# A four-block attention and scan kernel: the scan block's 64 prefix tokens computed in an own pass beside the first two stages

## The chip, the core and the metric

The kernel runs on one core of a Trainium2 chip. A core has TensorE (PE in the profile; its weight loads are the row PEld), VectorE (DVE), ScalarE (ACT), GpSimd (POOL) and SyncE (SP, which issues most DMAs here). Each engine works through its own queue in order; semaphores make an operation wait for others. SBUF is the on-chip memory of 128 partitions, PSUM the smaller one that PE writes its results to. The metric is device time in microseconds (us): the median of 3 runs is 4272.25 (4264.49 to 4274.65).

## The reference

Four blocks in a row on x of 4 sequences x 512 tokens x 256 features, all in float32:

- Block 0: cross-attention (16 heads of 16) to a context of 64 tokens, then a feed-forward part.
- Block 1: self-attention (16 heads of 64), cross-attention, gated feed-forward part, each after a layer norm.
- Block 2, the scan block: a prefix of 64 tokens, computed from the context alone, is put ahead of the 512 tokens, and four layers of a selective state-space scan run over all 576. At the end the prefix is dropped.
- Block 3: self-attention (16 heads of 16), cross-attention, feed-forward part.

The part that matters:

```
p = silu(prepend_cond @ pre_w1) @ pre_w2            # 64 prefix tokens, from the context alone
h = concatenate([p, x], axis=1)
for l in range(4):
    h = h + mamba_block(rmsnorm(h, norm_w[l]), ...)
return rmsnorm(h, final_norm_w)[:, 64:, :]

# mamba_block, E = 512 channels e, 16 states s
xi, z = split(x @ in_proj);  xi = silu(conv4(xi) + cb)     # causal, 4 taps
dt, Bm, Cm = split(xi @ x_proj);  dt = softplus(dt @ dt_proj + b)
h_t = exp(dt_t * A) * h_(t-1) + dt_t * Bm_t * xi_t         # for each e and s
y_t = sum over s of h_t * Cm_t + xi_t * D
return (y * silu(z)) @ out_proj
```

The scan is causal, so the prefix tokens never depend on x. What the 512 tokens need of the prefix is, for each layer, the state after its last token (h at token 63, for each channel and state) and the last three inputs of the convolution.

## The kernel before

Tokens lie on partitions in blocks 0, 1 and 3 (X, 16 tiles of 128 tokens), features in the scan block (hT, 2 chunks of 128 features x 4 sequences x 576 tokens). Line numbers are those of the profile.

**Blocks 0 and 1.** `cross_stage` (L348) and `self_stage` (L530) write out the order of the work by hand. A `Pieces` object (L59) holds small pieces, each a group of matmuls on PE and an eviction that reads their PSUM bank; `work` (L78) issues the matmuls of the next piece, `evict` (L70) the evictions of those issued before. The self-attention goes through 64 groups of four 128x512 score tiles (and 4 more iterations for what trails). One iteration k: PE transposes half of group k-1 (L668, copied to SBUF by ACT at L671), then makes the scores of group k (L627); DVE takes the row maxima (L642) and ACT the exponentials (L646); PE multiplies with the values (L687) and does a piece; PE transposes the other half of k-1, which DVE copies (L673); DVE divides the exponentials of group k by their sums, in SBUF (L654, L656); PE multiplies and does another piece. POOL only raises variances to the power -1/2 for the layer norms (L311) and adds biases to X (L815). The eight big weights of blocks 0 and 1 pass through six slots of 1 MB (pool w8): Wq1, Wk1, Wv1 and Wo1 are loaded during block 0, Wq2 and Wk2 when W1 and W2 are done with, Wv2 and Wo2 at the end of the self-attention, Wpa, Wpg and Wf after it.

**Scan block** (`layer2`, L942). 16 units n, one for each layer and sequence; each has two pairs of channel chunks, and each pair 16 main steps: two chunks times 8 groups of two states. The main steps i run through all units without a stop, and one of them is, spread over the engines:

```
nc.gpsimd.tensor_mul(dBu[:, :, 1:], dtx ..., bmap[i // 2, 0][:, :, 1:])            # L1385, POOL
nc.scalar.activation(dA, dt[:, S:], AF.Exp, scale=A[:, l, m, s : s + 1])           # L1397, ACT, into PSUM
nc.scalar.copy(dBus[i][:, :, 0], h0[:, 2 * s2 : 2 * s2 + 2])                       # L1402, ACT
nc.vector.tensor_tensor_scan(to, dA, dBus.pop(i) ..., 0.0, ALU.mult, ALU.add)      # L1412, DVE
nc.vector.tensor_mul(hCs[i], dA, bmap[i // 2, 1])                                  # L1419, DVE, 3 of 4 steps
nc.gpsimd.tensor_mul(hCs[i], hCs[i], bmap[i // 2, 1])                              # L1423, POOL, 1 of 4 steps
```

PE then sums over the states by transposing into one PSUM tile (L1445). The rows of B and C that these need reach all partitions by DMAs from a scratch tile in DRAM (`maps`, L1378). Beside the main steps, generators advance twice a step: `front` (norm, input projection, convolution as four matmuls with diagonal weights, B, C and dt) for the unit after next, `step` for the next pair, `gate` and `gated` for z, the product with silu(z) and the output projection with its residual add (L1362). Two PSUM banks are shared among them through `need`, `bank` and `done`.

The prefix goes through all this as 64 more columns: projections and convolution work on two halves of 288 columns (L1096, L1107, L1127, L1203), and `step` holds the prefix scan of each chunk: 16 exponentials of 64 columns (L1228, ACT), dt·x·B as one product of 128x1040 (L1230, POOL), one scan of 128x1040 (L1237, DVE), both of whose operands lie in SBUF, and a copy of the last state (h0, L1245, POOL). In layers 0 to 2 there are also the product with C (L1248, POOL), its sum over states on PE (L1261), a gate (L1317, L1326) and 64-column matmuls for z and the output projection. The prefix embedding itself (L1012 to L1017) opens the block.

## Time and profile before

| what | value |
|---|---|
| median of 3 runs | 4272.25 us |
| the profiled execution's own time | 4271.5 us |
| its span, first to last instruction | 4269.7 us |
| block 0 (0 to 266 us): PE / DVE / ACT / POOL busy | 222.7 / 117.1 / 67.2 / 62.8 us |
| block 1, self-attention (266 to 930 us) | see the prediction |
| block 1, cross-attention (930 to 1160 us) | 196.4 / 123.1 / 48.1 / 6.0 us, clock 0.96 |
| block 1, feed-forward (1160 to 1350 us) | 180.9 / 50.9 / 32.1 / 21.3 us |
| scan block, lead-in (1350 to 1430 us) | 64.9 / 10.0 / 35.3 / 14.8 us |
| scan block, main steps (1430 to 3515 us) | see the prediction |
| block 3 (3570 to 4270 us) | 609.3 / 411.9 / 314.3 / 73.4 us |
| scan block: distance of the products with silu(z) (L1460), one for each pair | 65 us mostly, 48.5 to 68.1 |

The profile is of one execution. A group's line gives the source line, engine, operation, the tiles (output <- inputs), the shapes, how many; then the busy time in us and the mean duration of one in ns; then the engine's idle time just before these instructions and what ended most of it. The line of a source line gives durations as minimum/median/maximum. A line of the timeline gives start, duration, engine, source line and tiles, and in brackets the idle time ahead of it. An f32 matmul shows as two records, a transpose as one. The granted clock is the share of TensorE's full clock that its throttle passed.

### The profile page before, as it was taken

What the parts mean: (1) busy time and instruction counts of PE and PEld (TensorE: products, weight loads), DVE (VectorE), ACT (ScalarE), POOL (GpSimd) and SP (SyncE); (2) the same over time, 40 slices, a digit from 0 to 9 for tenths busy, and PEclk for the clock granted to TensorE, in tenths of its full rate; (3) what the DMA queues carried; (4) which work ended last, traced back from release to release, by engine and by line L of the source; (5) the groups of instructions that cost most, each with busy time, mean ns of one, the idle gap of its engine ahead of it and who ended that gap; (6) DMA issues with size and microseconds to landing.
All of it is one profiled execution on the core that took longest, in us unless ns stands there. A gap on an engine that the chain in (4) does not pass through costs nothing. (4 is left out here: it accounts for less than half of the span.)

```text
span 4269.7 us, 51401 instructions
## 1 busy us (share of the span) xinstructions
PE 3642.0 (85%) x19008; PEld 2467.8 (58%) x19008; DVE 3086.3 (72%) x3120; ACT 2336.6 (55%) x5236; POOL 2146.8 (50%) x1204
## 2 busy tenths in 40 slices
PE   7999999988899788888887888888878567888789
PEld 3555555556556566666666666666656444545446
DVE  5536666664521599999999999999998986666653
ACT  2334445431212777777776777767777644555322
POOL 2300000010000799999999999999888971000131
PEclk8999999999999888889888898888888668999999
DMA  2000000010000344344344443444443431000000
GB/s 97 1 19 1 1 1 1 8 41 1 2 0 11 112 147 142 137 145 150 122 149 135 141 157 121 147 138 137 159 139 120 157 104 54 1 1 1 1 6 15
DMA packets 102378, 322.53 MB, mean 76 GB/s; under 512 B 12848, under 2 KB 28784, under 8 KB 100080
## 3 DMA queue, kind: packets, MB, share of 16 engines
q1 hardware_dynamic: 100048, 317.04, 22.4%
q8 instruction: 151, 2.47, 0.2%
q10 hardware_dynamic: 2080, 2.20, 0.2%
q14 instruction: 99, 0.81, 0.1%
HBM read 315.92 MB, written 3.28 MB: 75 GB/s over the span
## 5 line engine op out<-in xcount | busy, mean ns | idle before, releaser
L1385 POOL TENSOR_TENSOR dBu<-dtx,bB 128x1022 f32<-128x1022 f32 x512 | 1282.5, 2524 | 18.1 <-DVE ps_dA L1412 10.9
L1397 ACT ACTIVATE ps_dA<-dt,A 128x512 f32<-128x512 f32 x1024 | 706.7, 690 | 442.1 <-DVE hC L1419 399.3
L1412 DVE TENSOR_TENSOR_SCAN ps_dA<-ps_dA,dBu 128x1024 f32<-128x1024 f32 x384 | 877.3, 2285 | 52.8 <-ACT ps_dA L1397 24.3
L1445 PE MATMUL ps_y<-ident,hC 128*128 128x128 f32 x3072 | 472.2, 307 | 48.8 <-DVE hC L1419 48.4
L1419 DVE TENSOR_TENSOR hC<-ps_dA,bC 128x1024 f32<-128x1024 f32 x384 | 469.1, 1222 | 25.3 <-PE ps_y L1445 0.4
L1445 PEld LDWEIGHTS ps_y<-ident,hC 128*128 128x128 f32 x3072 | 414.5, 162 | 103.4 <-DVE hC L1419 72.3
L646 ACT ACTIVATE pr<-ps_s,nm 128x512 f32<-128x512 f32 x512 | 344.8, 685 | 233.1 <-DVE nm L642 233.1
L642 DVE TENSOR_REDUCE nm<-ps_s 128x2 f32<-128x1024 f32 x256 | 301.5, 1219 | 207.9 <-PE ps_s L627 186.9
L1423 POOL TENSOR_TENSOR hP<-hP,bC 128x1024 f32<-128x1024 f32 x128 | 301.6, 2356 | 79.9 <-DVE hP L1412 77.7
L160 PE MATMUL ps_cv<-xp,w_dg 128*128 128x288 f32 x1024 | 305.3, 457 | 37.0 <-ACT xp L1127 24.9
L311 POOL TENSOR_TENSOR ln_rstd<-ln_rstd,const 128x4 f32<-128x4 f32 x20 | 20.3, 1016 | 594.6 <-DVE ln_rstd L310 539.2
L1412 DVE TENSOR_TENSOR_SCAN hP<-ps_dA,dBu 128x1024 f32<-128x1024 f32 x128 | 292.1, 2282 | 30.0 <-PE ps_y L1445 28.5
L668 PEld LDWEIGHTS ps_pt<-ident,pr 128*128 128x128 f32 x2048 | 233.6, 141 | 136.8 <-issue 81.6
L668 PE MATMUL ps_pt<-ident,pr 128*128 128x128 f32 x2048 | 275.8, 276 | 33.9 <-DVE pT L673 22.1
L160 PEld LDWEIGHTS ps_cv<-xp,w_dg 128*128 128x128 f32 x1024 | 216.9, 217 | 117.8 <-issue 19.3
L1237 DVE TENSOR_TENSOR_SCAN hp<-dAp,hp 128x1040 f32<-128x1040 f32 x64 | 244.0, 3813 | 54.3 <-ACT dAp L1228 49.8
L1228 ACT ACTIVATE dAp<-dt,A 128x64 f32<-128x64 f32 x1024 | 282.0, 338 | 0.0
L208 POOL MEMSET Vbd<- 128x1024 f32 (+1 forms) x3 | 5.4, 1804 | 490.9 <-PE ps_wo L160 490.9
L687 PE MATMUL ps_o<-pT,V 128*64 128x256 f32 (+1 forms) x2048 | 220.0, 391 | 0.0
L160 PE MATMUL ps_in<-hn,w_inx 128*128 128x288 f32 x512 | 164.8, 467 | 56.6 <-DVE hn L1096 51.9
L673 DVE COPY pT<-ps_pt 128x512 f32<-128x512 f32 x256 | 164.5, 682 | 58.9 <-PE ps_pt L668 58.3
L1445 PE MATMUL ps_y<-ident,hP 128*128 128x128 f32 x1024 | 159.4, 307 | 55.5 <-POOL hP L1423 55.5
(239 smaller groups left out, 6541.1 us busy)
## 6 DMA issues: line engine op xcount, KB each, us to landing
bB<-scr SPq DMA_DIRECT2D x256, 512.0 KB, 5.0
bC<-scr SPq DMA_DIRECT2D x256, 512.0 KB, 4.1
bc<-scr SPq DMA_DIRECT2D x16, 1040.0 KB, 6.6
X<-in_x SPq DMA_DIRECT2D x4, 512.0 KB, 7.1
w_L_W<-in_L_W SPq DMA_DIRECT2D x2, 1024.0 KB, 10.4
w_L_Wq<-in_L_Wq SPq DMA_DIRECT2D x2, 1024.0 KB, 9.0
w_L_Wo<-in_L_Wo SPq DMA_DIRECT2D x2, 1024.0 KB, 10.6
w_inx<-in_L_in SPq DMA_DIRECT2D x4, 512.0 KB, 6.1
```

The costliest lines, as they stand in the source:

```text
L160: nc.tensor.matmul(dst, a, b, start=(i == 0), stop=(i == n - 1))
L642: nc.vector.tensor_reduce(nm, ps, AX.X, ALU.max, negate=True)
L646: nc.scalar.activation(pr, ps[:, x, :], AF.Exp, bias=nm[:, x : x + 1], accum_out=rs[:, y : y + 1])
L668: nc.tensor.transpose(pp[:, t4, :], pr[:, t4 * P : (t4 + 1) * P], ident)
L1228: nc.scalar.activation(dAp[:, s, 1:], dt[:, 1:S1], AF.Exp, scale=A[:, l, m, s : s + 1])
L1237: nc.vector.tensor_tensor_scan(hpf, dAp.rearrange("p s t -> p (s t)"), hpf, 0.0, ALU.mult, ALU.add)
L1385: nc.gpsimd.tensor_mul(dBu[:, :, 1:], dtx[:, S1:].unsqueeze(1).broadcast_to([P, 2, T - 1]), bmap[i // 2, 0][:, :, 1:])
L1397: nc.scalar.activation(dA, dt[:, S:], AF.Exp, scale=A[:, l, m, s : s + 1])
L1412: nc.vector.tensor_tensor_scan(to, dA, dBus.pop(i).rearrange("p s t -> p (s t)"), 0.0, ALU.mult, ALU.add)
L1419: nc.vector.tensor_mul(hCs[i], dA, bmap[i // 2, 1])
L1423: nc.gpsimd.tensor_mul(hCs[i], hCs[i], bmap[i // 2, 1])
L1445: nc.tensor.matmul(y[:, j, k * P : (k + 1) * P], hC[:, s, j * P : (j + 1) * P], ident, is_transpose=True, start=False, stop=(2 * s2 + s == ...
```

## The change

The prefix tokens leave the scan block. A generator, `prefix_pass`, computes all four layers for the prefix tokens of all four sequences at once (256 columns), keeps the state after token 63 (h63) and the last three convolution inputs (tail), and is advanced in small turns from inside the cross-attention stage of block 0 and the self-attention of block 1. The scan block then works on 512 columns: its projections use one PSUM bank instead of two halves; the convolution's first three columns come from tail; the state at its start is exp(A·dt) h63 + dt·x·B for 16 states, in one ACT operation and three small POOL operations a chunk; silu is flushed at steps 10 and 15 of a unit.

The pass's matmuls are pieces of a queue of their own (`aside`), with a PSUM tile from the tag of the transposes (self-attention) or of the projections (block 0). The main turn of the pass and how it is called, cut to the core:

```
+        def product(i):                                  # POOL, 128x512
+            nc.gpsimd.tensor_mul(hb, dtx[:, m, :].unsqueeze(1).broadcast_to([P, 2, PT]), maps.pop((i, 0)))
+        def decay(i):                                    # ACT, 2 of 128x256
+            nc.scalar.activation(dA[:, s, :], dt[:, m, :], AF.Exp, scale=A[...])
+        def scan(i):                                     # DVE, 128x512, both operands in SBUF
+            nc.vector.tensor_tensor_scan(hb, dA, hb, 0.0, ALU.mult, ALU.add)
+        def behind(i):
+            nc.scalar.copy(h63[:, l, :, m, 2 * q : 2 * q + 2], hb...[:, :, :, S - 1])
+            if not more:                                 # more: layers 0 to 2
+                return
...
+            nc.gpsimd.tensor_mul(hb, hb, bC)
+            nc.gpsimd.tensor_add(ys[m], ys[m], hb)
...
+        for i in range(NB + (4 if more else 3)):         # NB = 32
+            if i < NB: product(i)
+            if i + 1 < NB: load(i + 1, 0)                # SP, 256 KB to all partitions
+            if more and 0 <= i - 2 < NB: load(i - 2, 1)
+            if 0 <= i - 1 < NB: decay(i - 1)
...
+            if 0 <= i - 2 < NB: scan(i - 2)
+            if 0 <= i - 3 < NB: behind(i - 3)
+            to().busy = i < NB + 2
+            yield
```

(Conditions that stand on two lines in the kernel are written on one here.) Its convolution is one multiply-add with bias and three multiply-adds on DVE for each chunk, over 256 columns. The tiles for xi, z, dt and dt·x lie in hT, which is free until the scan block. In the self-attention:

```
                 evict()
+                todo.go_on(1)
                 back = k and k <= K
                 if back:
                     transposes(k - 1, 0)
+                todo.work_aside()
                 if k < K:
                     scores(k)
                     softmaxed(k)
                 through_values(lead // 2)
+                evict(0)
+                if k % 2 or not todo.busy:
+                    todo.go_on(1)
+                todo.work_aside()
                 work()
                 evict()
                 if back:
                     transposes(k - 1, 1)
+                todo.go_on(1)
+                todo.work_aside()
+                through_values(lead // 2)
+                evict(0)
                 if k < K and wide:
                     divided(k)
-                through_values(lead // 2)
                 work()
```

After the last iteration, what is left of the pass is run to its end. In block 0 the stage takes one turn in each of its 19 iterations and one after every second of the 32 feed-forward matmul groups: 35 in all.

To make room in SBUF, the weight pool has four slots instead of six: two hold block 0's gelu outputs first, so Wq1, Wk1, Wv1 and Wo1 wait for the slots of W1, W2 and these; Wk2 and Wv2 are loaded at the end of the self-attention; Wq2, Wo2 and Wf get a pool of their own that is opened when the pass's memory is free, after the self-attention. In block 0 the norm of the attention output is written over it instead of into a tile of its own. A is computed at the start of the program.

In the scan block, of `step`:

```
-                    hp = pool.tile([P, NS, S1], F32, name="hp", tag="hp")
-                    for s in range(NS):
-                        nc.scalar.activation(dAp[:, s, 1:], dt[:, 1:S1], AF.Exp, scale=A[:, l, m, s : s + 1])
-                        if s == 3:
-                            nc.gpsimd.tensor_mul(hp, dtx[:, :S1]..., bc0[:, 0])
...
-                    nc.vector.tensor_tensor_scan(hpf, dAp..., hpf, 0.0, ALU.mult, ALU.add)
...
+                    nc.scalar.activation(h0, A[:, l, m, :], AF.Exp, scale=dt[:, 0:1])
+                    yield
+                    nc.gpsimd.tensor_mul(i0, b0, dtx[:, 0:1].broadcast_to([P, NS]))
+                    nc.gpsimd.tensor_mul(h0, h0, h63[:, l, b, m, :])
+                    nc.gpsimd.tensor_add(h0, h0, i0)
+                    nc.scalar.copy(dt[:, 0:1], far)
```

`prefix_sum` and `prefix_gated` are gone, and so are the 64-column matmuls for z and the output projection, and the 1 MB load of the prefix's B and C for each unit.

## The prediction

> **What bounds the kernel now.** I read the busy time by stretches first, since shares over the whole span mix stages with different limits. The columns are the stretch, its length, then busy us (instructions) of PE, PEld, DVE, ACT and POOL, the granted clock, the DMA share and GB/s.
> ```profile
> 266.00:930.00 664.00, 649.06 (x3320) 356.43 (x3320) 416.91 (x797) 312.95 (x763) 31.39 (x33) 1.00 0.03 9
> 1430.00:3515.00 2085.00, 1684.58 (x8693) 1298.39 (x8691) 1925.14 (x1152) 1512.14 (x3401) 1921.66 (x943) 0.84 0.42 139
> ```
> The first stretch is the first self-attention: PE is busy 649 of 664 us and POOL does nothing. The second is the scan block: DVE and POOL are both busy 92%, PE 81%. So work moves from a stage that DVE and POOL bound into one that PE bounds. Next, the groups of instructions, for what the prefix costs where it is.
> ```profile
> L1385 POOL TENSOR_TENSOR dBu<-dtx,bB 128x1022 f32<-128x1022 f32 x512 | 1282.5, 2524 | 18.1 <-DVE ps_dA L1412 10.9
> L1237 DVE TENSOR_TENSOR_SCAN hp<-dAp,hp 128x1040 f32<-128x1040 f32 x64 | 244.0, 3813 | 54.3 <-ACT dAp L1228 49.8
> L1228 ACT ACTIVATE dAp<-dt,A 128x64 f32<-128x64 f32 x1024 | 282.0, 338 | 0.0
> ```
> The prefix scan (L1237) means 3.81 us, while the main scan of nearly the same length (L1412) means 2.28. The timeline of DVE, then of POOL, at one such scan says why:
> ```profile
> 2200.45 3.52 DVE L1237 TENSOR_TENSOR_SCAN hp<-dAp,hp 128x1040 f32<-128x1040 f32 x1
> 2203.90 2.27 DVE L1412 TENSOR_TENSOR_SCAN ps_dA<-ps_dA,dBu 128x1024 f32<-128x1024 f32 x1
> ```
> ```profile
> 2199.43 2.37 POOL L1385 TENSOR_TENSOR dBu<-dtx,bB 128x1022 f32<-128x1022 f32 x1
> ...
> 2201.77 4.35 POOL L1385 TENSOR_TENSOR dBu<-dtx,bB 128x1022 f32<-128x1022 f32 x1
> ```
> The scan starts at 2200.45, ends 2.2 us after POOL's product ends (2201.8), and the next product lasts 4.35 instead of 2.36: they take turns. All 42 products over 2.5 us lie beside an L1237 scan. The main scan, which reads one operand from PSUM, never shows this. Last, one step of the self-attention (PE and DVE of the timeline):
> ```profile
> 502.42 1.04 PE L668 MATMUL ps_pt<-ident,pr 128*128 128x128 f32 x8
> ...
> 504.56 2.35 DVE L642 TENSOR_REDUCE nm<-ps_s 128x2 f32<-128x1024 f32 x2 [1.87 <-PE ps_s L627]
> ...
> 508.77 1.29 DVE L673 COPY pT<-ps_pt 128x512 f32<-128x512 f32 x2 [1.86 <-PE ps_pt L668]
> ...
> 511.16 0.88 DVE L656 TENSOR_SCALAR pr<-pr,rs 128x512 f32<-128x512 f32 x2
> 511.94 1.04 PE L668 MATMUL ps_pt<-ident,pr 128*128 128x128 f32 x8
> ```
> A step takes 9.5 us, and DVE ends its division (L656) just as PE needs it: DVE has two gaps of 1.9 us, both waits for PE.
>
> **Scan block: removed.** It has 16 units (4 layers x 4 sequences) of 2085/16 = 130.3 us; DVE is busy 1925/16 = 120.3 of each. Out of each go four L1237 scans, 244.0/16 = 15.25, less 0.08 each that the trace lets overlap: 14.9; the prefix gate (L1326, 24 x 0.27/16 = 0.4); the 64-column residual add (24 x 0.21/16 = 0.3); and four 288-column norm products of 0.50 become two of 512 at some 0.75 (L913, same operation and width): 0.5. DVE keeps 104.2. POOL keeps 120.1 - 8.8 (L1230) - 7.1 (L1248) - 42 x 2.0/16 = 5.2 (products no longer held up) - 1.4 (shorter dtx, no h copy) + 2.4 (12 tiny operations at the h copy's 0.20) = 100.0, plus its 9.7 idle: less than DVE, so DVE stays the bound. ACT loses 17.6 a unit, PE its prefix sums. DVE's 10 us idle a unit: waits for ACT's decays (24.3 us in all) and for dtx (14.9) should shrink, waits for PE's out-projection (39.9) stay. I take 8, so a unit is 112.2 and the block loses 18.1 x 16 = **290 us**. Bounds: idle 5 (-338) and 12 (-226).
>
> **Lead-in of the block.** The prefix embedding between 1343.6 and 1353.7 goes (10 us), and of the 24 us from the end of the first softplus (1403.7) to the first main product (1427.6), with 32 exps and two scans, some 4 stay. I take **-30**; bounds -15 and -38.
>
> **Added: how much work, and where it falls.** A layer of the pass has 32 main steps (36 turns, with the pipeline's ends) and 13 or 14 turns of projections. In the cross block there are 35 turns, and there a projection costs two turns: 22 go for embedding and head of layer 0, 13 for main steps. The self-attention gets 3 turns an iteration, 2.5 while main steps run: 23+36+36 = 95 three-product turns (38 iterations), 35 of the last layer (14), 40 others (13.4). That is 65 of 68 iterations, so nothing is left over; a turn left over would run bare, 4.7 us.
>
> **A main turn.** POOL: product, product with C, sum, each 128x512. L1423 has 128x1024 at 2.36, so 1.18 each (L467, 128x512 with a broadcast, 1.04): 3.54; in the last layer 1.18. DVE: one scan of 512 with both operands in SBUF, half of L1237's shortest 2.31: 1.16. ACT: two exps of 256 (between 0.34 at 64 and 0.69 at 512) and a copy at 0.19: 1.0; ACT has 3 us to spare in a step.
>
> **The step under main turns.** PE adds nothing, so PE would still allow 9.8 (the stage's mean; 9.5 above). But what takes turns is 2.5 x (3.54 + 1.16) = 11.75, plus the step's own four divisions (L656, 0.44 to 0.485: 1.94) and POOL's bias adds (31.4/64 = 0.5): 14.2 us. That the divisions take turns too is read from one case: 0.98 instead of 0.48, beside the only bias add that overlaps one.
> ```profile
> L656 DVE TENSOR_SCALAR pr<-pr,rs x256: 473/484/977, 279.4 to 883.6; 128x512 f32<-128x512 f32 x128
> ```
> Behind a waiting division stand PE's next transposes, and behind a waiting scan the row maxima that ACT's exps need. So 38 x (14.2 - 9.8) = +167. In the last layer the shared work is only 8.3; DVE's own 6.5 + 2.9 and some waits make about 10.8: 14 x 1.0 = +14. Heads: 13.4 iterations with PE's share. All projections of the pass are 120 f32 matmuls of 256 columns, two records each at 0.243 (ps_wo, 139.9/576): 58 us, and 8 for means and broadcasts; 48 fall here, 17 in the cross block. The 16 convolution operations a layer (0.45 each, L316's 256 columns) stand in DVE's queue ahead of row maxima, and Silu and Softplus cost ACT four table loads of 1.28: some 2.1 an iteration. 48 + 28 = +76. **Self-attention: +257.** Bounds: if the turns fit DVE's gaps, 11.5 a step, +155; if each of the 6.5 SBUF-only DVE operations waits out a whole POOL operation, 9.4 + 6.5 x 1.18 = 17.1, about +377.
>
> The Trainium skill, "SBUF — State Buffer", section "Who interferes with whom", speaks against this change: GpSimd and VectorE share one port pair, held for a whole instruction, by VectorE operations with two SBUF inputs or in a two-port mode. By it the divisions (two-port, float32 in SBUF) always take turns and the sum is the 14.2 above; if the one 0.98 were chance, it would be 12.3 and the stage 74 us shorter. The same skill, "TensorE: Matmul & The Clock Gate", section "What's actually happening", adds that PE falls to half clock when it idles: this stage's 1.00 would not last.
>
> On the clock the rows say 1.00 at 98% busy, 0.96 at 85% (the first block's cross-attention) and 0.84 at 81%. At 0.90 a step's PE work is 10.9, still under 14.2; only heads and last layer would feel it, at most 1.1 x 27 = 30 us, kept in the range.
>
> **Cross block: +17** (its PE matmuls; PE is busy 223 of 266 us there; bounds +5 and +40). Two waits are new in it and lie in those bounds: the norm of the attention output now overwrites it, so DVE's scaling waits for POOL's residual add (0.76, behind up to 3.54 of a turn), with row maxima queued behind it; and ACT computes A (cols lands at 5.1, then a table load of 1.28) before it issues the row loads, which land 6.4 us later, near the first use of bv at 12.2. **Weights: +6.** Four slots instead of six: Wk1 waits for W2's last reader at 260 and is first read at 271.6; such loads land in 5.7 to 13.4 us. Wq2, Wo2, Wf wait for the pass's memory at the end of the self-attention. Bounds 0 and +20. The map loads (two of 256 KB a turn; 512 KB lands in 5.0 now) wait on SP only for slots that the turn before frees: nothing.
>
> **Sum.** -290 - 30 + 257 + 17 + 6 = -40 on this execution's 4271.5 us (span 4269.7): **4231 us**. The median, 4272.25, is 0.75 higher, which does not matter.
>
> **Rivals.** (a) *The cover holds*: POOL falls behind by up to its four buffers and the turns find DVE's two gaps; 11.5 us a step. For it: the gaps are there. Against: shared work is 14.2. Time 4271.5 - 320 + 155 + 23 = 4130. (b) *DVE starves behind POOL in the self-attention*: 17.1 us a step, -320 + 377 + 23 = +80: 4351, slower. For it: one L1237 scan lasted 6.97, behind two POOL operations. Against: most waited for one. It decides from 15.2 us a step, where 38 x 5.4 + 90 + 23 is about 320. (c) *The scan block gives less*: idle stays and grows because DVE and POOL feed each other; 118 us a unit, -197 - 20 + 280 = +63: 4335. Units above 114.7 make the whole slower. For it: in the last layer, where POOL already does 7 us less, units took 126 to 131, hardly less.
>
> **How the numbers follow.** Forecast 0.48, (a) 0.17, (b) 0.23, (c) 0.12. A measurement tells 0.3%, 13 us. The forecast's own bounds leave 0.34 faster, 0.08 same, 0.06 slower; (a) is faster; (b) 0.03 same, 0.20 slower; (c) 0.02, 0.02, 0.08. Together 0.53, 0.13, 0.34. Both signs hold much, so: the likeliest case alone spans 4190 to 4275; the range, taking in most of the rivals, 4130 to 4345.
>
> **What would show it.** g writes (L1460) 56 us apart instead of 65; the self-attention some 920 us long instead of 664; its divisions at about 1 us instead of 0.485, the prefix scan at 1.7 to 2.0 instead of 1.16, POOL busy some 350 us there. Wrong if the step stays under 12 us or passes 15, or a unit misses 109 to 115.

## The result and the profile after

The changed kernel takes **4426.88 us** (median of 4 runs, 4421.31 to 4432.11), the kernel before 4271.81 beside it: a ratio of **1.0366 [1.0347, 1.0384]**. The change costs 155 us; the forecast was a gain of 40, with 4130 to 4345 as the range. The profiled execution took 4421.31 us (span 4419.5), 149.8 more than the profiled one of before, and all sums below are made between these two. Against the forecast's gain of 40 that is 190 us worse: 159 of them are missing in the main steps of the scan block, 27 in its lead-in.

Split at the same instructions in both traces (first and last row maximum of the self-attention, first score tile of block 1's cross-attention, the seventh of the first eight transposes into the scan block, first and last main scan), the time goes as follows. "Measured" is after minus before.

| stage | before | after | measured | predicted |
|---|---|---|---|---|
| to the first row maximum (block 0, weights) | 275.5 | 293.9 | +18.4 | +17 and +6, with the next two rows |
| self-attention | 604.1 | 866.5 | **+262.4** | **+257** |
| to the cross-attention of block 1 | 56.4 | 60.8 | +4.4 | in +6 |
| cross-attention and feed-forward of block 1 | 402.3 | 400.0 | -2.3 | 0 |
| lead-in of the scan block | 97.2 | 94.1 | **-3.1** | **-30** |
| main steps of the scan block | 2072.5 | 1941.7 | **-130.8** | **-290** |
| rest | 761.7 | 762.5 | +0.8 | 0 |

So the cost came as foretold, and less than half of the gain. First the two stretches of the profile that answer to the two shown of before (columns: stretch, length, busy time of PE, PEld, DVE, ACT, POOL, granted clock, DMA share, GB/s):

```profile
294.00:1160.00 866.00, 698.16 (x3320) 373.95 (x3316) 724.16 (x902) 440.78 (x1141) 446.88 (x315) 0.94 0.22 68
1712.00:3664.00 1952.00, 1453.52 (x6616) 970.79 (x6617) 1679.51 (x1014) 1199.48 (x2176) 1616.37 (x956) 0.82 0.42 140
```

In the self-attention DVE is now busy 84% and PE 81%, where PE had 98% before. In the main steps every engine has become idler: DVE fell from 92% to 86%, POOL from 92 to 83%, PE from 81 to 74%. Work left the stage and the stage did not close up behind it. Next the groups that answer to the three of before, and two new ones of the self-attention:

```profile
L1541 POOL TENSOR_TENSOR dBu<-dtx,bB 128x1022 f32<-128x1022 f32 x512 | 1195.3, 2358 | 159.7 <-DVE ps_dA L1568 103.7 <-DMA bB<-scr 55.8
L518 DVE TENSOR_TENSOR_SCAN phb<-pdA,phb 128x512 f32<-128x512 f32 x128 | 199.4, 1559 | 5.5 <-issue 3.2 <-ACT h L523 2.2
L508 POOL TENSOR_TENSOR phb<-hT_res,pm 128x512 f32<-128x512 f32 x128 | 195.3, 1529 | 103.8 <-ACT h L523 55.5 <-DVE pT L972 16.9 <-DMA pm<-scrp 10.9
```

L1237 and L1228 are gone. POOL's main product (L1541) takes 2.358 us on average instead of 2.524, as foretold: no scan holds it up. But it now waits 103.7 us for the buffers that the main scan frees, where it waited 10.9 before. So POOL waits for DVE. (It also waits 55.8 us for the DMA of B's rows, 4.5 before: some 4 us at most, 16 times in all. DVE in turn waits only 6.7 us for POOL's products, so this is not what holds DVE.) What does DVE wait for? The list of its waits in the main steps, after and then before (waiting, for whom: us in total, times, longest):

```profile
DVE hT_res L1518 <- PE ps_out L177: 87.5, 30, 3.3
DVE ps_dA L1568 <- ACT ps_dA L1553: 67.5, 32, 3.7
DVE hn L1371 <- PE ps_rb L1366: 36.3, 14, 3.0
```
```profile
DVE hT_res L1362 <- PE ps_out L160: 39.9, 18, 3.5
DVE hP L1412 <- PE ps_y L1445: 28.5, 28, 3.1
DVE ps_dA L1412 <- ACT ps_dA L1397: 24.3, 21, 1.6
```

DVE's idle time (length less its busy time, first to last main scan) was 152.1 us and is 266.9. The three largest waits are those of the output projection's residual add, of the main scan for ACT's exponentials, and of the norm's product; the first and the third lie outside the main chain. Here is the first kind in DVE's timeline, then PE's at the same place:

```profile
2593.45 0.69 DVE L1518 TENSOR_TENSOR hT_res<-ps_out,hT_res 128x512 f32<-128x512 f32 x1 [2.57 <-PE ps_out L177]
2594.06 2.29 DVE L1568 TENSOR_TENSOR_SCAN ps_dA<-ps_dA,dBu 128x1024 f32<-128x1024 f32 x1
2599.48 0.69 DVE L1518 TENSOR_TENSOR hT_res<-ps_out,hT_res 128x512 f32<-128x512 f32 x1 [3.13 <-PE ps_out L177]
```
```profile
2588.00 1.98 PE L177 MATMUL ps_z<-w_inz,hn 128*128 128x512 f32 x4 [1.50 <-ACT zs L1488]
2589.82 3.60 PE L177 MATMUL ps_out<-gT,w_out 128*128 128x512 f32 x8
```

The add needs 0.69 us and holds DVE for 2.57 and 3.13: it is queued two half-steps after its matmuls were, and PE has z's matmuls ahead of it (1.98) and then 3.60 of its own.

### The profile page after: what moved, and what is told of

Its sections match the earlier page's. It is cut to its first block, busy times and chain, and to the rows that moved or that the text cites. A ratio compares the mean times of both kernels' runs of the same rounds, so it can differ in the third digit from the quotient of the medians.

```text
span 4419.5 us, 47894 instructions
## 1 busy us (share of the span) xinstructions
PE 3526.8 (80%) x17104; PEld 2177.6 (49%) x17104; DVE 3214.2 (73%) x3205; ACT 2202.5 (50%) x4456; POOL 2335.5 (53%) x1565
## 5 line engine op out<-in xcount | busy, mean ns | idle before, releaser
L1541 POOL TENSOR_TENSOR dBu<-dtx,bB 128x1022 f32<-128x1022 f32 x512 | 1195.3, 2358 | 159.7 <-DVE ps_dA L1568 103.7
L1568 DVE TENSOR_TENSOR_SCAN ps_dA<-ps_dA,dBu 128x1024 f32<-128x1024 f32 x384 | 877.8, 2286 | 93.1 <-ACT ps_dA L1553 67.5
L967 PE MATMUL ps_pt<-ident,pr 128*128 128x128 f32 x2048 | 294.7, 284 | 128.8 <-DVE pr L955 69.8
L177 PE MATMUL ps_cv<-xp,w_dg 128*128 128x512 f32 x512 | 237.0, 605 | 22.5 <-ACT xp L1393 18.9
L955 DVE TENSOR_SCALAR pr<-pr,rs 128x512 f32<-128x512 f32 x256 | 249.4, 1015 | 4.5
L508 POOL TENSOR_TENSOR phb<-hT_res,pm 128x512 f32<-128x512 f32 x128 | 195.3, 1529 | 103.8 <-ACT h L523 55.5
L1601 PEld LDWEIGHTS ps_y<-ident,hP 128*128 128x128 f32 x1024 | 142.9, 166 | 190.5 <-POOL hP L1579 165.2
L926 PE MATMUL ps_s<-kT,qT 64*128 64x512 f32 (+1 forms) x1024 | 218.1, 666 | 2.9 <-ACT kT L1168 2.1
L518 DVE TENSOR_TENSOR_SCAN phb<-pdA,phb 128x512 f32<-128x512 f32 x128 | 199.4, 1559 | 5.5 <-issue 3.2
L1590 PE MATMUL ps_y<-w_dD,xi 128*128 128x128 f32 x512 | 115.7, 417 | 102.5 <-DVE g L1617 102.5
L970 ACT COPY pT<-ps_pt 128x512 f32<-128x512 f32 x256 | 141.6, 589 | 110.2 <-PE ps_pt L967 110.0
```

What stands on the lines that cost most here:

```text
L177: nc.tensor.matmul(dst, a, b, start=(i == 0), stop=(i == n - 1))
L926: nc.tensor.matmul(ps[:, x, :], qs[c][q, i * P : (i + 1) * P], ks[c][q, :], start=True, stop=True)
L967: nc.tensor.transpose(pp[:, t4, :], pr[:, t4 * P : (t4 + 1) * P], ident)
L1541: nc.gpsimd.tensor_mul(dBu[:, :, 1:], dtx[:, 1:].unsqueeze(1).broadcast_to([P, 2, T - 1]), bmap[i // 2, 0][:, :, 1:])
L1568: nc.vector.tensor_tensor_scan(to, dA, dBus.pop(i).rearrange("p s t -> p (s t)"), 0.0, ALU.mult, ALU.add)
L1601: nc.tensor.matmul(y[:, j, k * P : (k + 1) * P], hC[:, s, j * P : (j + 1) * P], ident, is_transpose=True, start=False, stop=(2 * s2 + s == ...
```

## The experiments

Two names help. **The cover theory:** before, the prefix scan stood in holes that DVE's waits leave anyway; taken out, it gives back less than it took. **The rewrite theory:** the idle time is new, made by the whole-width projections and the order in which the rewritten scan block queues them. All ledgers below are split at the same instructions as the table above.

### s1: the kernel before, without the prefix scan

```
-                    nc.vector.tensor_tensor_scan(hpf, dAp..., hpf, 0.0, ALU.mult, ALU.add)      # L1237
```

> The kernel before, with only the prefix scan on VectorE (L1237, 64 of them, 244 us busy) left out of the scan block; the prefix states are then wrong. Busy theory: the block's main steps lose what VectorE loses, about 238 us, and the time falls to some 4035 us; the changed kernel's missing gain then comes from its new form. Filler theory: the prefix scan ran in part inside waits that VectorE has anyway (for ScalarE's silu lumps and TensorE's projections), so only 100 to 140 us come out: 4130 to 4170 us, and VectorE's idle time in the main steps rises above its 10 us a unit.

Measured: 4120.46 us, between the two theories' figures and close to the second's, the cover theory; main steps 1922.4 instead of 2072.5. From first to last main scan DVE is busy 226.8 us less (1693.6), and idle 76.7 us more (228.8): a third of what leaves is given back as waiting. First the stretch (columns as above), then the two largest waits of DVE:

```profile
1440.00:3362.00 1922.00, 1615.35 (x8657) 1256.56 (x8658) 1692.01 (x1087) 1505.08 (x3385) 1826.07 (x939) 0.86 0.45 151
```
```profile
DVE ps_dA L1408 <- ACT ps_dA L1393: 80.1, 65, 5.9
DVE hT_res L1358 <- PE ps_out L160: 67.5, 30, 3.4
```

These are the waits of the changed kernel, and here nothing was rewritten: 39.9 became 67.5 and 24.3 became 80.1 because the scan is out of DVE's queue. POOL, which keeps all its prefix work here, is busy 95% of the stretch, but DVE waits only 1.2 us for its products and 10.2 for dtx; by these rows it is not POOL that makes the new idle time. From here to the changed kernel DVE loses another 18.8 us of work (1693.6 to 1674.8) and gains 38.1 of idle time (228.8 to 266.9), so the rewrite makes the stage 19.3 longer. Both theories have a part, the cover theory the larger: 77 of the 115 us of new idle time.

### s2: the changed kernel, two adds later in DVE's queue

```
                     matmul_k(ps, [(w["out"] ...
                     yield
                     yield
+                    yield
+                    yield
                     ...
                     nc.vector.tensor_add(h, ps, h)                       # L1518
```

and the same two half-steps ahead of the norm's product (L1371).

> The changed kernel, with VectorE's residual add queued two half-steps later behind its output projection, and the norm product two half-steps later behind its broadcast. If those two waits (87.5 and 36.3 us of VectorE's idle time) are only a matter of where the operation stands in VectorE's queue, they go and the time falls by 80 to 120 us, to some 4310 to 4350. If TensorE's lateness itself paces the block, the wait moves to the next thing that TensorE frees (the slots of hC): less than 30 us.

Measured: 4330.44 us; main steps 1849.6, **92 us less** than in the changed kernel, by four empty half-steps.

```profile
DVE ps_dA L1572 <- ACT ps_dA L1557: 100.8, 72, 3.8
DVE ps_dA L1572 <- ACT dBu L1562: 25.0, 4, 23.7
DVE hT_res L1522 <- PE ps_out L177: 24.7, 30, 1.2
```

The residual add's wait falls from 87.5 to 24.7 and the norm's disappears from the list (the 25.0 is the stage's first step). So these waits were no lack of PE time: DVE was asked too early. DVE's idle time in the main steps falls to 174.5 us, and the largest wait left is that for ACT. (No run puts the later adds into s1, so how much of s1's new idle time is this same order of the queue stays open.)

### b2: the kernel before, the residual add two half-steps later

> The kernel before with the residual add of the 512 columns' output projection two half-steps later. Cover theory (before, the prefix scan stood in the holes that VectorE's waits leave; the wait for the output projection was 39.9 us there against 87.5 us in the changed kernel): the main steps lose at most those 40 us, 2030 to 2060 us, total 4232 to 4265 us. Rival (the waits are as dear in both kernels and before only showed them elsewhere): 60 us or more, main steps below 2010 us.

Measured: 4263.41 us beside 4273.71 (median of 7 runs); main steps 2064.2, 8.3 less. The wait for the output projection fell from 39.9 to 20.0, but DVE's for ACT's exponentials grew from 24.3 to 45.5. After, this edit took away the larger part of the waits that s2's 92 us consist of; before, it is worth 8, too little for a single run to tell from nothing, and DVE waits for ACT instead. The cover theory had allowed 12 to 40; the rival's 60 or more is out.

### s5, s6: what ACT is late with

Once a unit, ACT does silu of xi and of z together. In the changed kernel's timeline of ACT, and then of DVE:

```profile
2609.86 1.28 ACT L1632 ACT_TABLE_LOAD   x1
2611.15 1.91 ACT L1632 ACTIVATE xi<-xi 128x2048 f32<-128x2048 f32 x1
2612.97 1.90 ACT L1632 ACTIVATE zs<-zs 128x2048 f32<-128x2048 f32 x1
2614.88 1.28 ACT L1553 ACT_TABLE_LOAD   x1
```
```profile
2617.69 2.30 DVE L1568 TENSOR_TENSOR_SCAN ps_dA<-ps_dA,dBu 128x1024 f32<-128x1024 f32 x1 [3.70 <-ACT ps_dA L1553]
```

Such a lump of 6.4 us, once a unit, costs the main scan 3.70 (15 times in the changed kernel, 56 us; with s2's edit all 16, 59 us). Two edits on top of s2: z's copy one half-step later (s5), and silu of xi flushed alone at step 2 of the unit (s6).

```
-                    if main and r in (10, 15):
+                    if main and r in (2, 10, 15):                        # s6
```

> The changed kernel with the late adds, and in the scan block also the copy of z out of PSUM one half-step later. With the late adds ScalarE waited 68.3 us for z and 142.8 us for the convolution, and VectorE 100.8 us for ScalarE's exponentials. Theory (a late eviction on ScalarE makes the exponentials behind it late): z's part of that falls, the main steps go from 1850 to 1825 to 1840 us; if the silu of z then misses its step and comes with the next flush, they gain or lose up to 20 more. Rival (VectorE's waits for ScalarE are the silu lump with its table loads alone): the main steps stay within 5 us of 1850.

> The changed kernel with the late adds, and the silu of xi flushed at step 2 of a unit, where VectorE also has the product of the state sums with silu(z) (1.21 us), instead of together with z's at step 10. In the changed kernel the joint flush is 6.4 us of ScalarE (table load 1.28, xi 1.91, z 1.90, table load 1.28), and VectorE stood 3.7 us at each, 16 times. Theory (the lump is longer than the cover that VectorE has in its queue): at step 2 a lump of 4.5 us is covered, at step 10 one of 4.5 costs about 2; main steps 1850 less 16 times 1.7, 1815 to 1830 us. Rival (it is ScalarE's total that counts, and two more table loads for each unit, 41 us in all, make it later): main steps 1855 to 1880 us.

Measured: s5 4339.30 us with main steps of 1846.8 (2.8 less): z's eviction is not what makes ACT late. (Its self-attention, whose code is that of s2, took 873.7 instead of 865.8: a stage may differ that much between two executions, so a single run says nothing under 10 us.) s6 4363.70 us with main steps of **1884.7, 35 more**. Half of my theory held: at step 10 the halved lump (two table loads and one silu, 4.47 us) costs 1.70 instead of 3.70. The other half fell: at step 2 DVE stands 3.77 us at xi's lump, where I had expected nothing, and the waits for ACT rise to 136.7. So what a lump costs depends on where it stands, and DVE's product with silu(z), which I had counted as cover, did not help there. What does cover such a lump stays open.

### s3: the lead-in

```
-                    if i in (first, -12) or ...
+                    if i in (first, -3) or ...                            # start of the second unit's front
```

The reason to try it stands in POOL's timeline of the changed kernel. The last of the small products that make unit 0's initial state ends at 1681.7; the first main product starts 22 us later:

```profile
1681.51 0.22 POOL L1468 TENSOR_TENSOR h<-h,i 128x16 f32<-128x16 f32 x1
1681.67 0.31 POOL L1388 COPY xp<-tail 128x3 f32<-128x3 f32 x2
1697.77 0.19 POOL L1388 COPY xp<-tail 128x3 f32<-128x3 f32 x1 [15.79 <-PE ps_cv L177]
1703.93 0.18 POOL L1388 COPY xp<-tail 128x3 f32<-128x3 f32 x1 [5.97 <-PE ps_cv L177]
1704.07 9.25 POOL L1541 TENSOR_TENSOR dBu<-dtx,bB 128x1022 f32<-128x1022 f32 x4
```

ACT's queue has the same front ahead of the first exponentials, and these are later still. ACT, then DVE:

```profile
1711.83 0.58 ACT L1393 COPY xp<-ps_in 128x512 f32<-128x512 f32 x1 [1.11 <-PE ps_in L177]
1712.43 1.28 ACT L1553 ACT_TABLE_LOAD   x1
1713.73 1.42 ACT L1553 ACTIVATE ps_dA<-dt,A 128x512 f32<-128x512 f32 x2
```
```profile
1715.36 2.30 DVE L1568 TENSOR_TENSOR_SCAN ps_dA<-ps_dA,dBu 128x1024 f32<-128x1024 f32 x1 [25.36 <-ACT dBu L1558]
```

> The changed kernel, with the second unit's front (norm, projections, convolution) started at step -3 instead of -12, so that GpSimd's first products no longer stand behind that front's copies. If that order is what kept the lead-in at 94 us, the first main scan comes some 20 us earlier and the time falls by about 20 us; if the lead-in has another cause, nothing changes; if the second unit then comes late, the first two units grow by as much.

Measured: lead-in 64.6 instead of 94.1, so **29.5 us** of it was the second unit's front standing in the queues ahead of unit 0's first main step: three-column copies on POOL, each behind a convolution on PE, and evictions on ACT. The run moves both, and in the changed kernel ACT's part ended last. The main steps grew by 16.0 (1957.7), as that front now runs beside them. Total 4417.82.

### a1, a2, a3, a4: the self-attention

Sorted by what a step (from one group's row maxima to the next's) holds, the self-attention of the changed kernel is 33 steps with two or more prefix scans of the layers with three POOL operations a turn (mean 14.7, median 13.9 us), 11 with two or more of the last layer's (11.3) and 19 others, with projections for the most part (13.4); above the 9.57 of before these make +170, +19 and +73. One step in DVE's timeline:

```profile
313.04 2.66 DVE L955 TENSOR_SCALAR pr<-pr,rs 128x512 f32<-128x512 f32 x2
315.61 0.15 DVE L953 RECIPROCAL rs<-rs 128x2 f32<-128x2 f32 x1
315.80 2.18 DVE L955 TENSOR_SCALAR pr<-pr,rs 128x512 f32<-128x512 f32 x2
317.91 2.28 DVE L518 TENSOR_TENSOR_SCAN phb<-pdA,phb 128x512 f32<-128x512 f32 x1
323.77 2.36 DVE L941 TENSOR_REDUCE nm<-ps_s 128x2 f32<-128x1024 f32 x2 [3.58 <-PE ps_s L926]
```

Two divisions take 2.2 to 2.7 us (0.88 before), a scan 2.28 (1.16 at its best), and the next row maxima wait 3.58 us for PE's scores. Four kernels, each the changed one with an edit of its own:

```
-                    nc.gpsimd.tensor_mul(hb, hb, bC); nc.gpsimd.tensor_add(ys[m], ys[m], hb)    # a1: left out
-                    nc.vector.tensor_scalar(prs[k, x], prs[k, x], rs[:, x : x + 1], None, ALU.mult)
+                    nc.scalar.activation(prs[k, x], prs[k, x], AF.Identity, scale=rs[:, x : x + 1])   # a2
-                    nc.gpsimd.tensor_add(ys[m], ys[m], hb)
+                    nc.vector.tensor_add(ys[m], ys[m], pend.pop(i))       # a3, one turn later; C's product goes over the C map
-                if more and i > NS // 2 and (i - 3) % (NS // 2) == 0: gated(...)
+                if more and i > NS // 2 + 4 and (i - 5) % (NS // 2) == 0: gated(...)    # a4, with a2's edit
```

> The changed kernel, whose prefix pass leaves out the product with C and the sum over states on GpSimd for all but the first group of states (the prefix outputs of layers 0 to 2 are then wrong). Shared-port theory: what takes turns in a step of the first self-attention falls from 14.2 to 8.3 us and VectorE's own 9.4 us with some waits make 10.9, so the stage loses about 120 us of its added 262: 4300 us. Rival, TensorE's added matmuls, its lower clock and the order on ScalarE pace the stage: under 40 us.

> The changed kernel with one edit in the self-attention: the division of the exponentials (four 128x512 a step, VectorE) is done by ScalarE with the reciprocal as its scale; the reciprocal stays on VectorE. Turn-taking theory (VectorE's divisions, its prefix scans and GpSimd's products get in each other's way, and that sets the step): four divisions of 1.0 us leave, so the median step goes from 13.8 to 12.0 to 12.6 us, the self-attention from 866 to 770 to 800 us, and GpSimd's 128x512 products from 1.45 to 1.53 us to about 1.35. Rival (ScalarE becomes late instead: it gets four more operations of about 0.6 us behind its exponentials, 446 us busy today): the step stays above 13.4 us. Total by the first 4345 to 4365 us, by the second 4400 or more.

> The changed kernel with one edit in the prefix pass: the sum over states (one add of 128x512 a turn in the first three layers) goes from GpSimd to VectorE, a turn later; GpSimd's product with C is written over the C map, so that it no longer waits for ScalarE's copy of the last state. Theory that GpSimd is the late engine in the main turns: 96 times 1.45 us leave it, the median step falls by 1.5 us to 12.3, the self-attention from 866 to 790 to 815 us. Rival (the two share one budget, and a 128x512 add is 0.5 us alone, 1.0 beside GpSimd, on VectorE, ahead of row maxima): the step falls by less than 0.7 us and the stage stays above 840. Total by the first 4370, by the second 4410 us.

> The changed kernel with the divisions on ScalarE, as in the run before, and the prefix pass's gate (two VectorE operations for each channel chunk, which wait for the sum over states) two turns later, with a second tile for the sum. In the run with the divisions on ScalarE a gate stood 5.27 us in VectorE's queue waiting for GpSimd's last add, and a step of 19 us fell on most gates, among steps of 10.7 to 11.3. Theory of the in-order wait: the seven or eight steps of 15 to 19 us fall to 11 or 12, the self-attention from 811 to 755 to 775 us, total 4315 to 4335. Rival (GpSimd is the limit there and the wait only shows its arrears): the steps stay, or their time turns up in the neighbours, stage 795 or more, total 4355 or more.

| kernel | time | stage | steps of three POOL operations, mean | division | prefix scan |
|---|---|---|---|---|---|
| after | 4426.88 | 866.5 | 14.7 | 1.015 | 1.56 |
| a1: no product with C, no sum in 7 of 8 turns | 4344.94 | 786.9 | 12.1 | 0.73 | 1.39 |
| a2: divisions on ACT | 4371.64 | 810.6 | 12.6 (median 11.0) | ACT 0.71 | 1.70 |
| a3: sum on DVE | 4437.60 | 884.4 | 15.1 | 0.85 | 1.42 |
| a4: a2, gate two turns later | 4380.24 | 816.6 | 11.9 | ACT 0.71 | 1.76 |

a1: with fewer POOL operations DVE's are shorter too, as turn-taking has it. The stage lost 80 us, between the theory's 120 and the rival's 40. a2: without divisions beside them the main steps have a median of 11.0, lower than expected, but POOL's operations stay what they were (1.50 to 1.52 us on average, where 1.35 was expected). The stage lands a little above the expected 770 to 800, as the steps with projections got longer (13.4 to 14.5); ACT now has the divisions there beside its own silu and table loads, which is the likely reason. a3 fell flat: POOL lost 130 us of work, DVE's busy time stayed (724.2 to 721.5), and the stage grew by 18. The add takes 0.66 us on DVE at its shortest, not the 0.5 of the expectation. The waits moved into POOL (72.3 us for the prefix scan) and DVE's queue had one operation more ahead of the row maxima. In a2 a few steps of 15 to 19 us stood out; DVE's timeline of a2 shows one:

```profile
368.58 1.47 DVE L544 SCALAR_TENSOR_TENSOR py<-hT_res,cols,py 128x256 f32<-128x256 f32 x1 [5.27 <-POOL py L539]
```

The gate stands 5.27 us at the head of DVE's queue until POOL has caught up. a4 puts it two turns later: these steps fall (main steps 25 us less in all), and the other steps take 31 us back, one more of them being among those with projections. Nothing is gained. The rival had the numbers right; whether for its reason, that POOL is the limit, this run does not show.

### c1 to c8: put together

c1 is s2 with a2 and a3. c2 is s2 with a4 and with the convolution's eviction queued after the next input projection. c3 is s2, a2, that eviction and s6's early silu; c4 is c3 with the second front at step -6.

> The changed kernel with three edits: the scan block's residual add and norm product wait two half-steps longer (as in the run with the late adds: 92 us less in the main steps), the self-attention's divisions are on ScalarE, the prefix pass's sum over states is on VectorE. If the two self-attention edits add up: step 10.8 to 11.5 us, stage 700 to 740 us, total 4426 - 96 - 140 = about 4190 us (4150 to 4230), faster than both kernels. If only one of the two counts: about 4260 us. If ScalarE becomes the late engine: stage above 800, total above 4265 us.

> The changed kernel with the late adds, the convolution's eviction in the scan block later too (after the next input projection instead of before it), the divisions on ScalarE and the gate two turns later. Stage by stage: self-attention as in the run with those two edits (755 to 775 us if the in-order wait is it), main steps 1850 us if the convolution's eviction costs nothing, 1810 to 1835 if the 142.8 us that ScalarE waited for it made its exponentials late. Total: 4330 of the late adds less 100 in the self-attention and 0 to 40 in the main steps, 4190 to 4235 us, faster than both kernels. If the steps of the self-attention stay, 4265 to 4280.

> The changed kernel with the late adds, the convolution's eviction later, the divisions on ScalarE and the early silu of xi, the gate where the change has it. Self-attention 805 to 815 us as with the divisions on ScalarE, lead-in 88, main steps 1825 by the lump theory, 1860 by the rival. Total 4240 to 4260 us by the first (faster than both kernels), 4275 to 4295 by the second.

> The same with the second unit's front begun at step -6 instead of -12. The lead-in's 88 us hold about 25 us in which the first product waits on GpSimd's queue behind that front's copies; begun at -3 it gave 29.5 us there and took 16 back in the main steps. Theory: some 15 us less in the lead-in, at most 8 more in the main steps, total 4 to 12 us below the run without it. Rival (the front's work has to be done anyway and VectorE waits for it later): no difference within 3 us.

| kernel | time | ratio to before | self-attention | lead-in | main steps |
|---|---|---|---|---|---|
| c1 | 4306.45 | 1.0076 [1.0059, 1.0093] | 835.9 | 92.4 | 1856.0 |
| c2 | 4278.01 | 1.001 [1.000, 1.002] | 809.7 | 87.8 | 1850.3 |
| c3 | 4298.69 | 1.0063 [1.0048, 1.0078] | 816.6 | 87.8 | 1868.2 |
| c4 | 4285.52 | 1.003 [1.0018, 1.0041] | 815.9 | 68.6 | 1876.7 |

None of the four reached the better figure expected of it. c1: a2 and a3 do not add up; beside a2's 56 us in the self-attention, a3's edit takes 25 back. c2: the later eviction of the convolution gains nothing (1850.3 beside s2's 1849.6), though ACT had waited 142.8 us for it: those waits did not set the end. c3: the early silu loses again (1868.2). c4 against c3 is the theory's: 19.2 us less in the lead-in, 8.5 more in the main steps, 13 in all.

For the last four I asked what sets the 33 main steps once the divisions are gone. All have s2, a2, the convolution's later eviction and the second front at step -6. c5 has the product dt x B on DVE, c6 in every second turn only; c7 writes POOL's product with C over the C map instead of over the states (and has five tiles for the states instead of four); c8 is c7 with c5's product.

```
-                nc.gpsimd.tensor_mul(hb, dtx[:, m, :]..., maps.pop((i, 0)))
+                nc.vector.tensor_mul(hb, dtx[:, m, :]..., maps.pop((i, 0)))        # c5, c8
-                    nc.gpsimd.tensor_mul(hb, hb, bC)
+                    nc.gpsimd.tensor_mul(bC, hb, bC)                                # c7, c8
```

> The changed kernel with the late adds, the convolution's eviction later, the second unit's front begun at step -6, the divisions on ScalarE, and in the prefix pass the product dt x B (128x512 a turn) on VectorE instead of GpSimd; C's product and the sum stay on GpSimd. The main turns were 20 turns of 4.7 us of GpSimd work, 94 of the 100 us of eight steps. Theory (GpSimd is the limit there, and the product, unlike the sum, waits for nothing of GpSimd's): GpSimd keeps 2 operations a turn, 7 us a step, the gates find it ready, steps of 10 to 11 us, self-attention 735 to 770 us, total 4190 to 4225 us, faster than both kernels. Rival (what counts is the sum of what the two do in SBUF, whoever does it, and VectorE's queue is in order): as the sum on VectorE, stage 815 or more, total 4262 or more.

> The same with the product on VectorE in every second turn only. Theory: GpSimd has 3.8 us a turn, 9.5 a step, no longer the limit but near it; self-attention 750 to 785 us, total 4205 to 4240 us. Rival: stage 810 or more, total 4260 or more.

> The changed kernel with the late adds, the convolution's eviction later, the second unit's front begun at step -6, the divisions on ScalarE, and in the prefix pass the product with C written over the C map instead of over the states (the sum reads it there), with five tiles for the states instead of four; all three operations stay on GpSimd. With the divisions on ScalarE GpSimd waited some 109 us of the stage for ScalarE's copy of the last state, which stands in ScalarE's queue behind exponentials and divisions. Theory (that wait is GpSimd's arrears at the gates): most of it goes, self-attention 810 to 765 to 790 us, total 4225 to 4250 us. Rival (GpSimd's wait is slack that the other engines leave it): stage 800 to 820, total 4255 to 4270, no more than 0.4% from the kernel before.

> The same with the product dt x B on VectorE. There GpSimd waited 208 us for ScalarE's copy, and VectorE's product 32 us for GpSimd. Theory (the copy in ScalarE's queue, not GpSimd's work, sets the main turns): steps of 10.5 us as in the last layer, self-attention 880 to 770 to 800 us, total 4230 to 4260. Rival (VectorE's share, in its queue ahead of the row maxima, is what lengthens the step): 850 us or more, total above 4300.

| kernel | time | ratio to before | self-attention | POOL busy in it | steps of three operations, mean |
|---|---|---|---|---|---|
| c5 | 4331.01 | 1.0137 [1.0122, 1.0152] | 880.5 | 258.6 | 14.7 |
| c6 | 4318.65 | 1.0108 [1.0091, 1.0125] | 861.9 | 353.0 | 13.9 |
| c7 | **4246.82** | **0.9936 [0.992, 0.9953]** | 795.9 | 445.9 | 12.2 |
| c8 | 4271.44 | 0.9997 [0.9988, 1.0007] | 818.9 | 280.0 | 12.7 |

The rival was right of c5 and c6. c7 and c8 came between theory and rival, c7's total within the theory's. In c5 POOL has 42% less to do than in a2 (445.9 us) and the stage is 70 us longer. Its largest wait there is:

```profile
POOL phb L534 <- ACT h L523: 208.0, 59, 8.3
```

ACT's copy of the last state (0.2 us) stands in ACT's queue behind exponentials and divisions. POOL's product with C overwrote the very tile that this copy reads, so it had to wait for it, and DVE's next product waited for POOL's tiles. With the product written elsewhere, and one tile more for the states, this wait is gone: c8 is 62 us shorter in this stage than c5. (No run has the one edit without the other.) In c7, where POOL's own product needs those tiles, POOL still waits 71.8 us for the copy, where c4 had 112.8. c7's stage is 15 to 20 shorter than a2's and c4's, more than such a stage was seen to vary, and **c7 beats both kernels, before by 0.6% and after by 4.1%** (4246.82 to 4426.88). Its self-attention and its main steps (columns as above):

```profile
299.00:1095.00 796.00, 690.76 (x3322) 368.04 (x3322) 495.82 (x651) 586.10 (x1393) 445.89 (x316) 0.95 0.25 74
1625.00:3484.00 1859.00, 1442.56 (x6635) 965.54 (x6634) 1673.02 (x1012) 1204.93 (x2179) 1614.67 (x959) 0.84 0.44 147
```

DVE's share still counts: c8 is 23 us longer than c7 in this stage with 166 us less on POOL. So neither POOL's work alone nor its sum with DVE's is the limit. That it is the order of the operations in the queues is shown for this one tile, and beyond it argued.

## Why the prediction was wrong, point by point

**Main steps, -290 (measured -130.8): the step that failed** is "I take 8, so a unit is 112.2 and the block loses 18.1 x 16". It has two terms. DVE's work was right: 104.2 a unit foretold, 1674.8/16 = 104.7 measured. Its idle time was not: 8 foretold (bounds 5 and 12), 266.9/16 = **16.7** measured. This one number is 139 of the 159 us missing (266.9 less 128); DVE's extra 0.5 a unit is 8, and 12.5 are the ends of the stretch that I had counted into the stage (2085 instead of 2072.5). My reason was that waits for ACT and for dtx shrink when these have less to do, and that the wait for PE stays. s1 showed the opposite: with only the scan taken out, waits for ACT went from 24.3 to 80.1 and for the output projection from 39.9 to 67.5. An idle time of before is what is left after the removed work has filled what it could, and I had read it as a property of the stage. s2 showed the rest: the order of the queue, not PE's share, made 92 us of it. With its two later adds the idle time is 10.9 a unit, within the bounds, and the main steps are 223 us shorter than before, about what the upper bound of idle had allowed (226). What remains unexplained is part of the waits for ACT (s2: 100.8, of which about 59 are the silu lumps).

**Lead-in, -30 (measured -3.1):** the exponentials and scans that I struck did go, and the first main step then stood behind another unit's front on POOL and ACT. I had listed what waits on the way to the first product, and not what else is queued ahead of it and of the first exponentials. s3: 29.5.

**Self-attention, +257 (measured +262.4): right in its sum and close in its terms.** Main turns +167 foretold, +170 measured (33 steps at 14.7, instead of 38 at 14.2; counting every step that holds any product with C or sum, 37 at 14.2); last layer +14 against +19; projections +76 against +73. The one case from which the prediction read that divisions take turns was no chance. Minimum, median and maximum of L955, in the view that the prediction showed for L656, are now:

```profile
L955 DVE TENSOR_SCALAR pr<-pr,rs x256: 473/1254/2542, 298.9 to 1167.5; 128x512 f32<-128x512 f32 x128
```

The fastest is as fast as before (473 ns), the median went from 484 to 1254. The mechanism is that of the rule in the Trainium skill, "SBUF — State Buffer", section "Who interferes with whom": the trace agrees in both directions (POOL's 128x512 operation takes 1.27 us alone in a2's timeline and 2.06 to 2.19 beside a scan). The sum left out that POOL waits for ACT's copy and DVE's gate for POOL, which c5 to c8 and a4 showed; by the count of 33 it came out right with these waits in place of some turns, which is luck. That moving an operation off POOL did not shorten the stage (a3, c5) also says that the sum of both engines' operations is no law here.

**Cross block +17, weights +6:** 18.4 + 4.4 - 2.3 = +20.5 measured against 23. The clock's term was kept in the range only: it fell to 0.94 here, with PE busy 81%.

**Rivals.** (c), "the scan block gives less", is what happened, past its size: 118 a unit foretold, 121.4 measured (1941.7/16), over its own point of decision at 114.7. Its reason was half wrong: DVE waits for POOL's products only 6.7 us in all; the waits are for PE and ACT. Its chance of 0.12 was too low, since the profile had shown its best sign: in the last layer units had lost hardly anything though POOL did 7 us less. (a) and (b) priced the self-attention at 11.5 and 17.1 us a step and were both wrong. (By its own step of 17.1, (b)'s +377 should be 38 x 7.3 + 90 = +367; nothing hangs on it.)

**The signs named ahead:** the distance between products with silu(z), foretold at half of 112.2, was 59.3 and 63.3 in turn; divisions of about 1 us and prefix scans of 1.7 to 2.0 came as 1.015 and 1.56, the second short of its range; POOL's busy time in the self-attention, foretold at 350, as 446.9, since its 128x512 operations took 1.45 to 1.53 us on average beside DVE's instead of the 1.18 I had counted. The unit of 109 to 115, outside which I had called the forecast wrong, was missed.

## What to carry to other kernels

Before counting work taken off the bounding engine as time won, ask what its in-order queue waits for at that place: an operation that fills a wait gives back only what lies over it. A kernel without the work, run for its time alone, tells this at once (here 150 us for 227). After such a change look through the queue again for every operation that stands ahead of the bounding chain's next instruction and is not ready: two adds asked for too early (92 us), the front of a later unit (29.5), a tile overwritten while another engine still has to read it (15 to 62, with one more tile).

## What the runs showed of the hardware beyond expectation

- Work moved from POOL to DVE can lengthen the stage in which both work: POOL busy 446 to 259 us, and 811 to 880 us of stage (a2 to c5); 62 of these us went again with one tile no longer overwritten and one tile more (c8).
- The granted clock stayed at 0.94 to 0.95 on average in a stage with PE busy 81 to 87% (after and c7), although single gaps of PE reached 6.8 and 7.2 us there; c5 had 0.91 at 82%.
- The same 128x512 division takes 0.71 us on ACT and 0.47 on DVE when undisturbed; beside POOL, DVE's median is 1.25, so ACT is the faster engine for it there.
- What DVE waits at a lump of ACT depends on its place as well as its length: 3.70 us at one of 6.4 us at step 10 of a unit, 1.70 at one of 4.5 us there, 3.77 at one of 4.5 us at step 2 (after and s6).
